# Layer 0's start: input in four transfers, idle products on the identity, constants of layer 1 later, SyncE in the source's order

## The chip, the cores and the metric

The kernel runs on one core of one Trainium2 chip. A core has a matrix engine (TensorE, PE), a vector engine (VectorE, DVE), an activation engine (ScalarE, ACT), a general one (GpSimd, POOL) and a sync engine (SyncE, SP) that mostly issues transfers (DMAs). Each engine works through its own list of instructions in order, and waits on semaphores that the other engines and the DMAs raise. The metric is the device time of one execution in microseconds (us); less is better.

## What is computed

Two transformer layers on an input of 4 sequences x 512 tokens x 256 features, all in float32:

```
x = x + L0_attn(layernorm(x))     causal attention, 16 heads of 16
x = x + L0_ffn(layernorm(x))      router over 8 experts per output feature, top 2
x = x + L1_attn(layernorm(x))     16 query heads of 128, 4 key/value heads
x = x + L1_ffn(layernorm(x))      gated MLP of 2048, weights unpacked from 4 bits
```

The change lies in the start of the first line: the layer norm, the projections to queries, keys and values, and the first scores of the attention.

```
_layernorm(x) = (x - mean(x)) / sqrt(var(x) + 1e-05)
qkv = einsum('bsd,od->bso', x, w_project)
att = softmax(where(causal, -1e9, q . k / sqrt(16)))
out = einsum('bsd,od->bso', att . v, w_out)
```

## The kernel before

The 2048 tokens lie in SBUF as `xres`, 128 partitions x 16 tiles x 256 features. Four tiles make a block (512 tokens); there are four blocks, and block j holds the same 128 positions of all four sequences. Layer 0's attention goes through 44 batches (`batches`): block 0 has four, one for each sequence, with all four groups of heads at once; block 1 has eight; the blocks 2 and 3 have sixteen each.

What every batch does is written as functions: `greatest(n)` computes scores on PE (L652), `mask(n)` adds the causal mask on PE and takes row maxima on DVE (L665, L671), `shift(n)` transposes the maxima and subtracts them from the queries (L681, L684), `powers(n)` computes scores again, exponentials on ACT and the causal cut on POOL (L700, L709, L719), `mixed(n)` multiplies with the values (L736). Between them `fill` takes pieces from other streams: projections of the next block, the folding of the router's biases into its weights (`fold_pieces`, L258, which reads the weights `rw` and `ew`), later the router and expert products.

The order of the work on PE, DVE, POOL and ACT is that of the source: `tc.manual_schedule` over these four engines (L72) is open from L72 to L1179. SP is not among them before the change: the framework's scheduler places its transfers, except that the expert weights' transfers keep their order among themselves (`load_pair`, L531). In the compiled list of SP, this leads to the order: half of block 0's input, half of the projection weights `wp`, block 1's input, `wo`, block 2's input, four transfers of `rw`, block 3's input, three of the biases `bs`, four of `ew`, then the transfers of queries and keys (`qk`) of block 0 (eight on SP, eight on ACT's queue), block 1's first eight, four of `rw`, eight of `qk`, four of `ew`.

The start, before the first batch, goes as follows.

- The input of block 0 is loaded in two transfers of two tiles each, one by SP and one by ACT (L65, L66), then `wp` in two halves (L460).
- POOL makes the identity `ident`; DVE makes small constants, among them `mask32` (L86), `fold8` (L91) and `mask8` (L95). The last two are used in layer 1 only. POOL writes `qk` blanks (L482, L486), `ident_h` and `later` (L489 to L492). DVE fills the values' ones (`va`, L481) and clears `bs` (L497), into which the biases are loaded (L499).
- PE computes three idle products of `ident` with `wp` (L800). Each float32 product is shown as two records.
- DVE takes statistics of four tiles (L180, L181), adds epsilon (L184), POOL takes the power -1/2 (L185), DVE normalizes the tiles (L194, `xn`); PE transposes (L210), ACT copies to `xT` (L582). The same norm follows at once for block 1.
- POOL: `blanks`, then `blank(1, i)` (L476, L474), then the split of the biases into three bfloat16 parts (`split_biases`, L518 to L529).
- `projections(0, xT)`: for each of two halves two products (`project`, L545), evicted by ACT into `stage` (L549) and sent by eight transfers into `qk` (L555), four issued by SP and four by ACT; then two value products (`values`, L567), evicted by ACT (L573). PSUM has two buffers for all of these (`ps_dn`, L100), so that a product waits for the eviction of the last but one.
- `inputs_T(1, ...)` transposes block 1 (copied by DVE, L582), then `greatest(0)`, `mask(0)`, and the batches begin.

Of the kernel before, what the change touches and what calls it, by code (L numbers as in the profile page):

```python
# [32 lines left out]
def tile_transformer(  # L33
# [40 lines left out]
    make_identity(nc, ident)  # L74
    minus_half = const.tile([P, 4], F32, name="minus_half")
# [19 lines left out]
    nc.vector.tensor_copy(mask8, fold8.unsqueeze(1).to_broadcast([P, NS, 8]))  # L95

# [352 lines left out]
    with ExitStack() as l0:  # L449
# [32 lines left out]
        nc.gpsimd.tensor_copy(  # L482
            qk[:, :, 0].rearrange("p g s q -> p g (s q)"),
            mask32[:, :4].unsqueeze(2).to_broadcast([P, 4, 512]),
# [45 lines left out]

        def load_pair(w, dram, n):  # L531
            e, hc = divmod(n, 2)
            tc.keep_in_program_order(
                nc.sync.dma_start(
                    out=w[:, hc, 2 * e : 2 * e + 2],
                    in_=dram[hc * P : (hc + 1) * P, 2 * e : 2 * e + 2],
                )
            )

        def project(j, xT, half, stage, i):  # L540

            at = 256 * (1 - i) + 128 * half
            ps = ps_dn.tile([P, 512], F32, tag="dn", name=f"qk_ps{j}_{half}_{i}")
            for hc in range(2):
                nc.tensor.matmul(  # L545
                    ps, lhsT=wp[:, hc, at : at + P],
                    rhs=xT[:, hc].rearrange("p s q -> p (s q)"), start=hc == 0, stop=hc == 1,
                )
            nc.scalar.copy(stage[:, i], ps)  # L549
            if i:  # L550
                to = 4 + j % 2
                for r in range(8):
                    h = 32 * (r % 4)
                    eng = nc.scalar if j == 0 and r % 2 else nc.sync
                    eng.dma_start(  # L555
                        out=qk[h + 4 : h + 20, 2 * half + r // 4, j : to + 1 : to - j].rearrange(
                            "p i s q -> p i (s q)"
                        ),
                        in_=stage[16 * r : 16 * r + 16],
                    )  # L560

        def values(j, xT, s):

            ps = ps_dn.tile([P, 2, HID], F32, tag="dn", name=f"v_ps{j}_{s}")
            for i in range(2):
                for hc in range(2):
                    nc.tensor.matmul(  # L567
                        ps[:, i], lhsT=xT[:, hc, s + i], rhs=wp[:, hc, 512:768],
                        start=hc == 0, stop=hc == 1,
                    )  # L570
            at = j * per_block
            to = va[:, at : at + per_block].rearrange("p (s h d) -> p s h d", s=NS, d=17)
            nc.scalar.copy(  # L573
                to[:, s : s + 2, :, 0:16], ps.rearrange("p s (h d) -> p s h d", d=16)
            )

# [13 lines left out]
        def projections(j, xT):  # L590
            if j > 1:
                for s in (0, 2):
                    yield need("PE", 1.75, 1, cond=lambda: blanked > 5 * j - 10)
                    values(j, xT, s)
            for half in range(2):
                if j > 1 and half:

                    stage = b1.tile(
                        [P, 2, 512], F32, tag="hi4" if j == 2 else "part", name=f"stage{j}_1"
                    )  # L600
                elif j or half:
                    stage = a1.tile([P, 2, 512], F32, tag="stage", name=f"stage{j}_{half}")
                else:
                    stage = unused("stage0", "p (i q) -> p i q", i=2)
                for i in range(2):

                    yield need(
                        "PE", 1.75, 0 if half or i else 1,
                        cond=lambda: j < 2 or done >= 8 * j - 12 and blanked >= 5 * j - 5,
                    )  # L610
                    project(j, xT, half, stage, i)
                if half == (not j) and j < 2:
                    for s in (0, 2):
                        yield need("PE", 1.75)
                        values(j, xT, s)

        def prepare(j):

            out = []
            yield from norm_pieces(  # L620
                j, b1, b2, out, cond=lambda: j == 2 or inputs[2].next is None
            )
            xT = a1.tile([P, 2, NS, P], F32, tag="xT0", name=f"xT0_{j}")
            yield from inputs_T(j, out[0], xT)
            yield from projections(j, xT)

        def unused(name, pattern, **sizes):
# [168 lines left out]


        ps = ps_mm.tile([P, 4, P], F32, tag="mm", name="idle")
        for i in range(3):
            nc.tensor.matmul(  # L800
                ps.rearrange("p b q -> p (b q)"), lhsT=ident, rhs=wp[:, 0, :512],
                start=not i, stop=i == 2,
            )
        load_x(1)
        nc.sync.dma_start(out=wo, in_=w_out.rearrange("(k p) o -> p k o", p=P))
        both = [[], []]
        for j in range(2):
            for piece in norm_pieces(j, b1, b2, both[j]):
                pass
            normed.clear()  # L810
            if not j:
                blanks(both[0][0])
                xT = a1.tile([P, 2, NS, P], F32, tag="xT0", name="xT0_0")
                for piece in inputs_T(0, both[0][0], xT):
                    pass
# [6 lines left out]
        for piece in inputs_T(1, both[1][0], xT):  # L822
            pass
        greatest(0)
        mask(0)
# [7 lines left out]
        for n in range(NBT):  # L833
# [473 lines left out]
```

## Time and profile before

| | us |
|---|---|
| median of 3 runs (1169.44 to 1170.32) | 1169.55 |
| the profiled execution's time | 1170.3 |
| its span | 1168.6 |
| PE busy | 1142.0 |
| DVE busy | 809.8 |
| ACT busy | 484.3 |
| POOL busy | 108.4 |
| first statistics of block 0 (DVE) | 5.96 |
| first projection of block 0 (PE) | 13.51 |
| first maxima of the first batch (DVE) | 28.79 |

The profile is of one execution. The span runs from its first instruction to its last; the profiled execution's own time is 1.7 us longer than its span and 0.75 us above the median. A row of the timeline has the start and the duration in us, the engine, the line of the source, the operation, its output and inputs, the shape and a count; the last bracket is the idle time of that engine before it and what ended the wait. Where several instructions are merged the duration is that from the first start to the last end. "PEld" is PE's loading of weights, "SPq" and "ACTq" are issues of transfers. In the rows of DMA issues "us to landing" is counted from the issue. The granted clock of PE in the profile is 1.00 in every stretch of 10 us looked at in the first 120.

### The profile page before, as it was taken

Reading aid. Unit: us, or ns where it says so; the run is one execution under the profiler, and the core shown is the slowest. Engines: PE = TensorE matmul, PEld = TensorE weight load, DVE = VectorE, ACT = ScalarE, POOL = GpSimd, SP = SyncE. Lnnn points to the kernel's source line nnn. Section 1 sums busy time; section 2 is a strip of 40 time slices with the busy share of each in tenths; the row PEclk is TensorE's granted clock in tenths of the full one; section 3 lists DMA queues with packets and bytes.
Section 4 is the critical chain, followed back from the end, with each engine's and each line's share of the span. In section 5 each row is a group of like instructions: output and inputs, shape, how many; then the busy total and the mean of one; then the engine's idle time right before and its main releaser. Section 6 shows DMA issues by size and latency. Waiting matters only on the chain.

```text
span 1168.6 us, 18563 instructions
## 1 busy us (share of the span) xinstructions
PE 1142.0 (98%) x7178; PEld 661.5 (57%) x7178; DVE 809.8 (69%) x1783; ACT 484.3 (41%) x1099; POOL 108.4 (9%) x152
## 2 busy tenths in 40 slices
PE   7999999999999999999999999999999999999998
PEld 3666555556554445555555555566644475484487
DVE  5676889999988953868773785687699845716710
ACT  1444645556555542444443444544344312303300
POOL 7322221212112000000000000000000000000000
PEclk9999999999999999999999999999999999999999
DMA  7230110000000500000000001120110000000000
GB/s 219 64 83 2 19 20 2 2 1 2 2 2 1 181 1 1 1 1 1 1 1 1 1 1 46 28 54 21 27 46 1 0 1 19 0 1 19 1 18 19
DMA packets 21239, 26.46 MB, mean 23 GB/s; under 512 B 5128, under 2 KB 14600, under 8 KB 21152
## 3 DMA queue, kind: packets, MB, share of 16 engines
q1 hardware_dynamic: 20480, 24.10, 7.5%
q10 hardware_dynamic: 672, 1.18, 0.4%
q8 instruction: 56, 0.92, 0.3%
q14 instruction: 31, 0.25, 0.1%
HBM read 18.97 MB, written 2.10 MB: 18 GB/s over the span
## 4 chain that ended last, share of the span: by engine, by line
PE 81%; DVE 13%; ACT 2%; issue 1%; POOL 1%; DMA 0%; SPq 0%; ACTq 0%; DVEq 0%; POOLq 0%
PE qk_ps L987 11%; PE y L1234 9%; PE o L1078 9%; PE g L916 9%; PE u L916 9%; PE lg_ps L234 8%; PE eo L234 7%; PE s L652 3%; PE s L700 3%; DVE mx L671 3%; PE av L736 2%; PE v_ps L969 2%; PE qk_ps L545 2%; PE a L1058 1%; PE s L1000 1%
## 5 line engine op out<-in xcount | busy, mean ns | idle before, releaser
L987 PE MATMUL qk_ps<-xT,wqkv 128*128 128x512 f32 x320 | 148.9, 599 | 2.3 <-ACT part L323 1.2
L234 PE MATMUL lg_ps<-rw,xT 128*128 128x512 f32 x256 | 122.5, 601 | 1.4 <-ACT xT L954 0.3
L234 PE MATMUL eo<-ew,xT 128*128 128x512 f32 x256 | 121.5, 600 | 0.8 <-ACT lg L297 0.5
L1078 PE MATMUL o<-wpj,oT 128*128 128x256 f32 x512 | 119.1, 382 | 0.0
L1234 PE MATMUL y<-wd,it 128*128 128x256 f32 x512 | 111.8, 379 | 0.0
L1078 PEld LDWEIGHTS o<-wpj,oT 128*128 128x128 f32 x512 | 95.9, 190 | 27.5 <-issue 14.3
L1234 PEld LDWEIGHTS y<-wd,it 128*128 128x128 f32 x512 | 97.0, 190 | 15.0 <-issue 2.2
L671 DVE TENSOR_REDUCE mx<-s 128x1 f32<-128x384 f32 (+3 forms) x176 | 100.4, 632 | 1.3 <-PE s L665 1.3
L987 PEld LDWEIGHTS qk_ps<-xT,wqkv 128*128 128x128 f32 x320 | 59.1, 190 | 71.4 <-issue 57.4
L709 ACT ACTIVATE pt<-s 128x512 f32<-128x512 f32 (+1 forms) x176 | 84.1, 563 | 35.3 <-PE s L700 35.3
L916 PE MATMUL g<-xT,wgu 128*128 128x512 f32 x192 | 90.4, 593 | 0.0
L916 PE MATMUL u<-xT,wgu 128*128 128x512 f32 x192 | 90.2, 592 | 0.0
L323 ACT ACTIVATE part<-eo,c 128x256 f32<-128x256 f32 x128 | 53.7, 472 | 85.2 <-PE eo L234 75.2
L719 POOL TENSOR_SCALAR_AFFINE_SELECT pt<-pt 128x256 f32<-128x256 f32 (+2 forms) x88 | 63.2, 725 | 249.8 <-ACT pt L709 249.3
L1212 ACT ACTIVATE th<-sq 128x512 f32<-128x512 f32 x64 | 40.3, 630 | 87.6 <-DVE sq L1211 87.6
L234 PEld LDWEIGHTS lg_ps<-rw,xT 128*128 128x128 f32 x256 | 46.1, 190 | 46.1 <-issue 37.3
L234 PEld LDWEIGHTS eo<-ew,xT 128*128 128x128 f32 x256 | 46.1, 190 | 45.7 <-issue 38.3
L222 DVE TENSOR_TENSOR xres<-xres,y 128x256 f32<-128x256 f32 x16 | 6.7, 421 | 92.5 <-PE y L1234 92.5
L185 POOL TENSOR_TENSOR ln_rs<-rs_v,minus_half 128x4 f32<-128x4 f32 x16 | 17.6, 1099 | 552.2 <-DVE rs_v L184 439.9
L297 ACT COPY lg<-lg_ps 128x512 f32<-128x512 f32 x64 | 37.6, 588 | 73.5 <-PE lg_ps L234 73.5
L1213 DVE SCALAR_TENSOR_TENSOR th<-th,g 128x512 f32<-128x512 f32 x63 | 43.2, 686 | 29.2 <-ACT th L1212 29.2
L916 PEld LDWEIGHTS u<-xT,wgu 128*128 128x128 f32 x192 | 36.5, 190 | 45.9 <-issue 44.7
(233 smaller groups left out, 1776.8 us busy)
## 6 DMA issues: line engine op xcount, KB each, us to landing
qk<-stage SPq DMA_DIRECT2D x56, 64.0 KB, 2.4
wqkv<-in_w_qkv SPq DMA_DIRECT2D x8, 320.0 KB, 6.8
rw<-in_router_w SPq DMA_DIRECT2D x8, 256.0 KB, 7.8
ew<-in_expert_w SPq DMA_DIRECT2D x8, 256.0 KB, 4.6
wpj<-in_w_proj SPq DMA_DIRECT2D x1, 2048.0 KB
out<-xres SPq DMA_DIRECT2D x4, 512.0 KB, 2.6
xres<-in_x SPq DMA_DIRECT2D x3, 512.0 KB, 9.0
dq_wgu<-in_gate_w SPq DMA_DIRECT2D x8, 128.0 KB, 2.4
```

The source lines that it names most:

```text
L234: nc.tensor.matmul(ps, lhsT=xT[:, hc, (g % 4) * P : (g % 4 + 1) * P], rhs=w[:, hc, 2 * pair : 2 * pair + 2, :].rearrange("p e o -> p (e o) ...
L297: nc.scalar.copy(lg[:, 2 * pair : 2 * pair + 2, :].rearrange("p e o -> p (e o)"), ps)
L323: nc.scalar.mul(part[:, e % 4], ps[:, i], c[:, e : e + 1])
L671: nc.vector.tensor_reduce(maxes[n % 2][:, h, gs[0] : gs[0] + nb], ps[:, : nb * nk].rearrange("p (b k) -> p b k", b=nb), AX.X, ALU.max,)
L709: nc.scalar.activation(pt[:, i, : nb * nk], tiles[2 * pair + i][:, : nb * nk], AF.Exp, scale=0.25)
L719: nc.gpsimd.affine_select(out=last, in_=last, compare_op=ALU.is_ge, fill=0.0, base=0, pattern=pattern, channel_multiplier=-1,)
L916: nc.tensor.matmul(ps, lhsT=wgu[:, w, half, jj, par * P : (par + 1) * P], rhs=xT[:, half, :], start=half == 0, stop=half == 1,)
L987: nc.tensor.matmul(ps, lhsT=wqkv[:, hc, kv, h, :], rhs=xT[:, hc, :], start=hc == 0, stop=hc == 1,)
L1078: nc.tensor.matmul(ys[t // 2][:, t % 2], lhsT=state["o"][:, h, t * P : (t + 1) * P], rhs=wpj[:, HPK * kv + h, :], start=kv == 0 and h == 0 ...
L1212: nc.scalar.activation(th, sq, AF.Tanh, scale=0.7978845608028654)
L1213: nc.vector.scalar_tensor_tensor(th, th, 1.0, gp, ALU.add, ALU.mult)
L1234: nc.tensor.matmul(ps, lhsT=it[:, c // 2, c % 2, t * P : (t + 1) * P], rhs=wd[:, c // 2, c % 2, :], start=c == 0, stop=c == 2 * NJ - 1,)
```

## The change

- Block 0's input goes in four transfers of one tile, by SP and ACT in turn.
- SP is put in the source's order too, from the constants on until batch 3 (`loads_in_order`); `load_pair` loses its own ordering.
- `fold8` and `mask8` are computed behind the evictions of block 0's values, ahead of the copies of block 1's `xT`.
- The idle products are five, of `ident` with `ident` repeated four times; they read no weights.
- Block 0's norm becomes `normed_by_twos`: statistics of two tiles, epsilon, POOL's power for those two, the same for the other two, then four `xn`.
- The clearing of `bs`, the biases' transfers and the filling of `va` come behind block 0's transposes in the source, so behind `xn` on DVE.
- Block 1's statistics are written ahead of block 0's projections of half 0, its `xn` behind them. PE's own order stays what it was.
- Block 0's projections of half 1 and its values are evicted by DVE, no longer by ACT. On DVE these four evictions stand behind block 1's `xn`.
- Block 2's input is loaded behind block 0's projections, block 3's in batch 2. As the loads now stand in source order, SP's list becomes: two tiles of block 0, half of `wp`, block 1's input, `wo`, three of `bs`, eight `qk` of block 0, block 2's input, eight `qk` of block 1, eight of `rw`, eight `qk`, four of `ew`, block 3's input, four of `ew`, and from there on as before.

```diff
-    for t, eng in ((0, nc.sync), (2, nc.scalar)):
-        eng.dma_start(out=xres[:, t : t + 2, :], in_=x[:, t : t + 2, :])
+    for t in range(4):
+        eng = nc.scalar if t % 2 else nc.sync
+        eng.dma_start(out=xres[:, t, :], in_=x[:, t, :])
...
+    loads_in_order = ctx.enter_context(ExitStack())
+    loads_in_order.enter_context(tc.manual_schedule(engines={mybir.EngineType.SP}))
...
-    nc.vector.tensor_reduce(
-        fold8, ident.rearrange("p (t b) -> p b t", b=8), AX.X, ALU.add
-    )
-    nc.vector.tensor_copy(mask8, fold8.unsqueeze(1).to_broadcast([P, NS, 8]))
...
-        nc.vector.memset(va[:, :per_block], 1.0)
...
-        nc.vector.memset(bs, 0.0)
-        for i in range(3):
-            nc.sync.dma_start(out=bs[32 * i : 32 * i + 8], in_=bias)
...
-            nc.scalar.copy(stage[:, i], ps)
+            (nc.scalar.copy if j or not half else nc.vector.tensor_copy)(stage[:, i], ps)
...
-            nc.scalar.copy(
+            (nc.scalar.copy if j else nc.vector.tensor_copy)(
                 to[:, s : s + 2, :, 0:16], ps.rearrange("p s (h d) -> p s h d", d=16)
             )
...
+        def normed_by_twos():
...
+            for two in (slice(0, 2), slice(2, 4)):
+                for t in range(two.start, two.stop):
+                    nc.vector.bn_stats(st[:, t, :], xres[:, t, :])
+                    nc.vector.bn_aggr(mv[:, t, :], st[:, t, :])
...
+                nc.vector.tensor_scalar(v, mv[:, two, 1], EPS, None, ALU.add)
+                nc.gpsimd.tensor_tensor(rs, v, minus_half[:, :2], ALU.pow)
+                roots.append(rs)
+            for t in range(4):
+                nc.vector.tensor_scalar(
+                    xn[:, t, :], xres[:, t, :], mv[:, t, 0:1],
+                    roots[t // 2][:, t % 2 : t % 2 + 1], ALU.subtract, ALU.mult,
+                )
...
-        for i in range(3):
+        for i in range(5):
             nc.tensor.matmul(
-                ps.rearrange("p b q -> p (b q)"), lhsT=ident, rhs=wp[:, 0, :512],
-                start=not i, stop=i == 2,
+                ps, lhsT=ident, rhs=ident.unsqueeze(1).to_broadcast([P, 4, P]),
+                start=not i, stop=i == 4,
             )
...
+        xn = normed_by_twos()
+        blanks(xn)
...
+        nc.vector.memset(bs, 0.0)
+        for i in range(3):
+            nc.sync.dma_start(out=bs[32 * i : 32 * i + 8], in_=bias)
+        nc.vector.memset(va[:, :per_block], 1.0)
+        second = []
+        norm_1 = norm_pieces(1, b1, b2, second)
+        for _ in range(3):
+            next(norm_1)
+        firsts_0 = projections(0, xT)
+        for _ in range(3):
+            next(firsts_0)
+        for piece in norm_1:
+            pass
...
-        for piece in projections(0, xT):
+        for piece in firsts_0:
             pass
+        load_x(2)
+        nc.vector.tensor_reduce(
+            fold8, ident.rearrange("p (t b) -> p b t", b=8), AX.X, ALU.add
+        )
+        nc.vector.tensor_copy(mask8, fold8.unsqueeze(1).to_broadcast([P, NS, 8]))
...
-            if n in (0, 2):
-                load_x(n // 2 + 2)
+            if n == 2:
+                load_x(3)
+            if n == 3:
+                loads_in_order.close()
```

More of the change, by code (lines that the diff above doesn't have):

```diff
@@ L532, in load_pair @@
             e, hc = divmod(n, 2)
[L533 to L537, printed above, removed]
+            nc.sync.dma_start(
+                out=w[:, hc, 2 * e : 2 * e + 2],
+                in_=dram[hc * P : (hc + 1) * P, 2 * e : 2 * e + 2],
             )
@@ L625, in prepare @@
             yield from projections(j, xT)
+        def normed_by_twos():
+            xn = b1.tile([P, 4, HID], F32, tag="xn", name="xn0_0")
+            st = b2.tile([P, 4, 6], F32, tag="ln_st", name="ln_st0_0")
+            mv = b2.tile([P, 4, 2], F32, tag="ln_mv", name="ln_mv0_0")
+            roots = []
+            for two in (slice(0, 2), slice(2, 4)):
+                for t in range(two.start, two.stop):
+                    nc.vector.bn_stats(st[:, t, :], xres[:, t, :])
+                    nc.vector.bn_aggr(mv[:, t, :], st[:, t, :])
+                v = b2.tile([P, 4], F32, tag="rs_v", name=f"rs_v0_{two.start}")[:, :2]
+                rs = b2.tile([P, 4], F32, tag="ln_rs", name=f"ln_rs0_{two.start}")[:, :2]
+                nc.vector.tensor_scalar(v, mv[:, two, 1], EPS, None, ALU.add)
[6 more added lines that the diff above has]
+                )
+            return xn
         def unused(name, pattern, **sizes):
@@ L805, in tile_transformer @@
         nc.sync.dma_start(out=wo, in_=w_out.rearrange("(k p) o -> p k o", p=P))
[L806 to L815, printed above, removed]
+        xn = normed_by_twos()
+        blanks(xn)
+        xT = a1.tile([P, 2, NS, P], F32, tag="xT0", name="xT0_0")
+        for piece in inputs_T(0, xn, xT):
+            pass
[11 more added lines that the diff above has]
+        for piece in norm_1:
+            pass
+        normed.clear()
         for i in range(5):
@@ L818, in tile_transformer @@
         split_biases()
-        for piece in projections(0, xT):
+        for piece in firsts_0:
             pass
+        load_x(2)
[3 more added lines that the diff above has]
+        nc.vector.tensor_copy(mask8, fold8.unsqueeze(1).to_broadcast([P, NS, 8]))
         xT = unused("xT0_1", "p (h s q) -> p h s q", h=2, s=NS)
-        for piece in inputs_T(1, both[1][0], xT):
+        for piece in inputs_T(1, second[0], xT):
             pass
```

## The prediction

> **What bounds the kernel now.** I read the page first, then the opening of the timeline, then the chain and the waits in the same stretch. The page says that the kernel is one long TensorE (PE) program:
>
> ```profile
> span 1168.6 us, 18563 instructions
> PE 1142.0 (98%) x7178; PEld 661.5 (57%) x7178; DVE 809.8 (69%) x1783; ACT 484.3 (41%) x1099; POOL 108.4 (9%) x152
> ```
>
> PE is busy 98% of the span, and the diff alters its list of instructions in one place only: three idle products become five. So nothing can be won from PE's work. What can be won is time ahead of it. The timeline of the first 32 us (start, duration, engine, line) shows that opening:
>
> ```profile
> 1.90 1.89 POOL L482 COPY qk<-mask 128x2048 f32<-128x2048 f32 x1 [0.53 <-DVE mask L86]
> 2.16 3.42 DVE L95 COPY mask<-fold 128x32 f32<-128x32 f32 x1
> 3.73 1.80 POOL L486 MEMSET qk<- 128x2048 f32 x1
> 5.96 0.36 DVE L180 BATCH_NORM_STATS2 ln_st<-xres 128x6 f32<-128x256 f32 x1
> 7.12 5.27 PE L800 MATMUL idle<-wp,ident 128*128 128x512 f32 x6 [7.12 <-DMA wp<-in_w_project]
> 8.40 1.02 POOL L185 TENSOR_TENSOR ln_rs<-rs_v,minus_half 128x4 f32<-128x4 f32 x1 [2.13 <-DVE rs_v L184]
> 9.46 1.38 DVE L194 TENSOR_SCALAR xn<-xres,ln_mv,ln_rs 128x256 f32<-128x256 f32 x4 [1.14 <-POOL ln_rs L185]
> 12.23 1.04 PE L210 MATMUL x_ps<-ident,xn 128*128 128x128 f32 x8
> 13.51 7.13 PE L545 MATMUL qk_ps<-xT,wp 128*128 128x512 f32 x16 [0.24 <-DMA xres<-in_x]
> 14.31 2.52 DVE L194 TENSOR_SCALAR xn<-xres,ln_mv,ln_rs 128x256 f32<-128x256 f32 x4 [1.13 <-POOL ln_rs L185]
> 20.91 1.07 ACT L549 COPY stage<-qk_ps 128x512 f32<-128x512 f32 x2 [3.08 <-DMA qk<-stage]
> 22.02 2.80 ACTq L555 DMA_DIRECT2D qk<-stage  x4
> 24.91 1.07 ACT L573 COPY va<-v_ps 128x512 f32<-128x512 f32 x2 [2.93 <-DMA qk<-stage]
> 26.63 1.81 PE L652 MATMUL s<-qk 32*128 32x128 f32 x32
> 28.79 2.48 DVE L671 TENSOR_REDUCE mx<-s 128x4 f32<-128x512 f32 x4 [1.26 <-PE s L665]
> ```
>
> Three losses are to be seen. The first statistics start at 5.96 although the two halves of the input were issued at 0.8 and took 4.0 to 4.2 us to land, so at about 5.0: VectorE (DVE) was held by the 128x32 copy of L95, which took 3.42 us and ended with POOL's memset (5.53). The transposes start at 12.23 although xn was ready at 10.84: six passes of idle products stand ahead of them, begun only when the projection weights had landed (7.12). And ScalarE (ACT) evicts the third projection and the values 3.08 and 2.93 us late, because it is issuing four DMAs each time. The chain names the same items: mask L95 for 3.42 us, then DMA qk<-stage for 3.00. From the first maxima (28.79) on, the order on PE and the waits are those of both kernels, so I carry the sum to that point and compare there.
>
> **The change, part by part.**
>
> *Input in four, DVE cleared.* Two more issues of 0.4 us; the weights wp are issued 0.42 later, land at about 7.4 instead of 7.0, and are needed after 10. DVE loses L91, L95 and both memsets ahead of the statistics and is free at 1.84, so the landing binds. The two halves, 0.5 MB, landed near 4.9; the DMA view of the first 30 us shows 376 GB/s in that stretch, so half the bytes are there 0.7 us sooner: an estimate of 4.2 for the first pair, 4.9 for the second. Four statistics with their aggregation take 2.15 us in the old timeline (5.96 to 8.11). In two pairs, each behind its transfer, they end near 6.6, the first pair at 5.4.
>
> *The root in two.* POOL's own queue is untouched: L482, L486, L489 to L492 end at 6.27. So the first root cannot start before 6.3, whatever the input does. One of 128x4 costs 1.02; one of 128x2 is not in the trace. It lies between half (0.5) and the full 1.02; I take 0.9, nearest to the measured row, so that the pair ends at 8.1 (7.3 to 8.4). Here a rule speaks against the split. The Trainium skill (SBUF — State Buffer, Who interferes with whom) says that a VectorE copy or tensor_scalar in its two-port mode and a GpSimd instruction exclude each other for a whole instruction. The row that bears on it: xn takes 1.38 for four at 9.46 with POOL idle and 2.52 at 14.31 beside four POOL copies. By an undisturbed row the first two xn would pass beside the second root and all four end at 8.8; by the rule they wait for it and end at 8.1 + 1.38 = 9.5. I take the rule: 9.5 (8.7 to 9.8).
>
> *Idle products on the identity.* Ten passes, which wait only for ident (1.4). The old six ran 0.86 us apart up to 12.2, twice the 0.43 of the projections, so PE came to full pace 4.4 to 5.1 us after its first product. With four to eight slow passes the ten end between 7.5 and 9.2: off the path, and cost nothing while xn is the later. If all ten stayed slow they would end at 10.0 and cost 0.5. In the chain block 2 shows 1.05 us between the end of its last xn (50.96) and its first projection (52.01). So the projections start at 9.5 + 1.05 = 10.55 instead of 13.51: 2.96 us won.
>
> *Memsets of bs and va moved behind xn.* On the chain they are worth 0.5 each, as rows 0.91 and 0.96: 1.0 to 1.9, I take 1.2. From the end of xn of block 0 to the start of xn of block 1 the old kernel needs 3.47 (10.84 to 14.31). So xn of block 1 runs from 9.5 + 1.2 + 3.47 = 14.2, with POOL's four copies beside it again (2.52), to 16.7. Queued behind it are the new evictions. The bias transfers wait for the memset of bs and stand ahead of the qk transfers on SP; they issue at about 10 to 11, the qk transfers not before 14.9.
>
> *Evictions of half 1 and of block 0's values to DVE.* The third projection is complete 5.45 us after the start: 16.0. DVE takes it at 16.7 (0.65, as its two xT copies at 26.25, 1.29) to 17.35. PE ends the fourth at 10.55 + 7.13 = 17.7 and finds the PSUM buffer free: no wait where the old one lost 0.9. DVE evicts the fourth to 18.45, the values run from 17.75 to 21.45 (3.72), their second eviction ends at 22.15, the transposes of block 1 at 22.75. ACT, with nothing but issues left, starts the second set of qk transfers at 18.45 instead of 22.02; the last of four is issued at 20.65, and with the median of 3.7 us to landing the last scores end near 24.9, with SP's 2.4 near 23.9. I take 24.5, and the first maxima on PE's side at 24.85.
>
> *fold8 and mask8 behind the evictions.* Reduction 0.37, to 22.5. The copy is the 3.42 row again. Uncontended it is under 0.1; here POOL is in the bias split (18.3 to 28.9 in the old timeline, instructions of 0.6 to 1.5). I wait for one of them, as each xn did, and take 1.2: 23.7. Two xT copies: 25.0. So the first maxima come at 25.0: **3.8 us earlier than 28.79**.
>
> *Loads in the source's order.* Nothing is added: 16 weight transfers, of which eight used to go at 3.5 to 15. Block 2's input now goes behind the second qk set (about 21) and is read at 43.9 - 3.8. rw goes behind the first qk transfers of block 1, from about 38.4; its first pair is added to at 54.2 - 3.8 = 50.4, and the longest landing of an rw or ew transfer in the trace is 8.0 after issue, so by about 47.5. ew follows the transfers at 54.7 to 59.8, so from 56; first use 71.5 - 3.8 = 67.7, landing by 65. Block 3's input lies between and is used near 94. Cost nothing, with 3 us of cover; what hides it is block 1's scores. If the cover went, DVE's L258 would hold the maxima queued behind it.
>
> **Sum.** 3.8 us off the profiled execution: its span 1168.6 becomes 1164.8, its time 1170.3 (1.7 around the span) becomes 1166.5. That execution is 0.75 above the median, so I forecast 1169.55 - 3.8 = **1165.8**. The unknowns: xn -0.8/+0.3, landing -0.6/+0.4, memsets up to +0.7, mask8 -1.1/+0.8. Together 1164.2 to 1167.2.
>
> **Rivals.**
>
> *PE cools down again* (9%). The skill (TensorE: Matmul & The Clock Gate, The HAM clock gate) says that the half rate returns after an idle window of about 3.4 us. Idle products that end at 7.5 leave 3.0 us with only transposes before 10.55. The old gap was 1.3 us (12.2 to 13.51), so the trace shows nothing either way. By the row no cost; by the rule in its bad phase 5.1 us at half pace, 2.5 us lost: 1168.3. I take the row, as the gap is under the window.
>
> *The gain is given back at the loads* (9%). If ew or rw land over 7 us later than reckoned, DVE waits at L258 and the start's 3.8 are lost: 1169.5, or beyond. Against it: the 8.0 was met under a heavier load (298 GB/s in the first 10 us) than there will be.
>
> *mask8 locked out to the end of the bias split: slower* (8%). The old copy sat through two POOL instructions. If it sits through all to 28.87, the xT copies end at 30.3 and the maxima start 1.5 us later than now: 1171.1. It decides from the point where mask8 ends after 27.5. Against it: POOL's split waits for its own results with gaps of 0.06 to 0.08, and xn alternated one for one with POOL at 14.31 and at 47.45.
>
> *Chances.* Forecast 74%; the change is measurable from about 0.2%, 2.3 us, so below 1167.2. Faster 0.76 (the forecast, and a mild case of cooling), same 0.19 (cooling, most of the loads' case, mask8), slower 0.05 (a loads' case worse than reckoned). The range 1164.2 to 1168.6 takes in the forecast and cooling.
>
> **What would show it.** First statistics near 4.2 and not 5.96; roots at 6.3, 7.2; xn ending at 9.5; projections at 10.55; values at 17.75 without a wait; ACT's second issues at 18.45; mask8 near 1 us; first maxima at 25.0; all later rows shifted by one constant; no DVE wait at L258. I am wrong if the projections' passes run 0.86 apart, if mask8 ends after 25, or if the shift at 100 us differs from that at 30.

## The result and the profile after

| | before | after |
|---|---|---|
| median (runs) | 1170.26 (12) | 1166.9 (12) |
| range of the runs | 1169.03 to 1170.85 | 1166.59 to 1169.71 |
| profiled execution, its span | 1170.3, 1168.6 | 1166.64, 1164.9 |
| first projection of block 0 | 13.51 | 9.60 |
| first maxima | 28.79 | 24.87 |

The ratio after to before is 0.9976 [0.9969, 0.9984]: 2.8 us faster by the ratio, 3.4 by the medians, 3.7 by the two profiled executions. Ten of the twelve runs lie between 1166.59 and 1167.00; the other two, 1168.25 and 1169.71, come back below. The forecast was 1165.8, range 1164.2 to 1168.6.

The head of the page of after, first its span and the busy time of each engine, then the granted clock in tenths over the span's 40 slices:

```profile
span 1164.9 us, 18575 instructions
...
PE 1144.1 (98%) x7182; PEld 662.6 (57%) x7182; DVE 812.4 (70%) x1788; ACT 481.9 (41%) x1095; POOL 108.2 (9%) x153
...
PEclk9999999999999999999999999999999999999999
```

PE has four records more (two idle products), and 2.1 us more of busy time in a span that is 3.7 shorter. The gain is time ahead of PE's work. The opening in the timeline of after (start, duration, engine, line; last bracket: idle time before it and what ended it):

```profile
1.43 6.68 PE L816 MATMUL idle<-ident 128*128 128x512 f32 x10 [1.43 <-POOL ident masks.py:199]
...
3.50 0.43 DVE L629 BATCH_NORM_STATS2 ln_st<-xres 128x6 f32<-128x256 f32 x1 [1.66 <-DMA xres<-in_x]
...
4.71 0.86 DVE L633 TENSOR_SCALAR rs_v<-ln_mv 128x2 f32<-128x2 f32 x1
...
6.26 1.51 POOL L634 TENSOR_TENSOR ln_rs<-rs_v,minus_half 128x2 f32<-128x2 f32 x2
...
7.00 1.54 DVE L637 TENSOR_SCALAR xn<-xres,ln_mv,ln_rs 128x256 f32<-128x256 f32 x4 [0.47 <-POOL ln_rs L634]
...
9.60 7.13 PE L539 MATMUL qk_ps<-xT,wp 128*128 128x512 f32 x16 [0.24 <-ACT xT L576]
...
13.99 6.41 SPq L549 DMA_DIRECT2D qk<-stage  x8
14.01 6.83 ACTq L549 DMA_DIRECT2D qk<-stage  x8
...
14.17 2.52 DVE L194 TENSOR_SCALAR xn<-xres,ln_mv,ln_rs 128x256 f32<-128x256 f32 x4 [1.12 <-POOL ln_rs L185]
...
16.61 1.27 DVE L543 COPY stage<-qk_ps 128x512 f32<-128x512 f32 x2
...
17.34 3.72 PE L561 MATMUL v_ps<-wp,xT 128*128 128x256 f32 x16 [0.60 <-DVE stage L543]
...
22.11 1.41 DVE L850 COPY mask<-fold 128x32 f32<-128x32 f32 x1
...
22.43 2.08 PE L668 MATMUL s<-qk 32*128 32x128 f32 x32
...
24.87 2.48 DVE L687 TENSOR_REDUCE mx<-s 128x4 f32<-128x512 f32 x4 [0.16 <-PE s L681]
```

Two things are to be seen against the opening of before. Nothing now stands between the last xn and its transposes: the idle products end at 8.11, xn at 8.54, the projections follow 1.06 later, 3.91 us earlier than in before. And the shift is nearly the same further on. PE waits 0.60 at the values, where before waited 0.91, because the third eviction stands on DVE behind block 1's xn; so the values start 4.21 earlier, and the scores 4.20. The scores then take 2.08 us and not 1.81, which brings the shift to 3.92 at the first maxima; the trace shows no wait of PE in them. From there it stays: 3.92 at the products of 107.83 us in before (103.91 in after), 3.83 at the last addition.

### The profile page after: what moved, and what is told of

The parts are those of the page before. It is cut to its first block, busy times and chain, and to the rows that moved or that the text cites. A ratio compares the mean times of both kernels' runs of the same rounds, so it can differ in the third digit from the quotient of the medians.

```text
span 1164.9 us, 18575 instructions
## 1 busy us (share of the span) xinstructions
PE 1144.1 (98%) x7182; PEld 662.6 (57%) x7182; DVE 812.4 (70%) x1788; ACT 481.9 (41%) x1095; POOL 108.2 (9%) x153
## 4 chain that ended last, share of the span: by engine, by line
PE 82%; DVE 13%; issue 2%; ACT 1%; POOL 1%; SPq 0%; DMA 0%; POOLq 0%; DVEq 0%; ACTq 0%
PE qk_ps L1019 11%; PE y L1266 9%; PE o L1110 9%; PE g L948 9%; PE u L948 9%; PE lg_ps L234 8%; PE eo L234 7%; PE s L668 3%; PE s L716 3%; DVE mx L687 3%; PE av L752 2%; PE v_ps L1001 2%; PE qk_ps L539 2%; PE a L1090 1%; PE s L1032 1%
## 5 line engine op out<-in xcount | busy, mean ns | idle before, releaser
L687 DVE TENSOR_REDUCE mx<-s 128x1 f32<-128x384 f32 (+3 forms) x176 | 100.5, 633 | 0.2 <-PE s L681 0.2
L185 POOL TENSOR_TENSOR ln_rs<-rs_v,minus_half 128x4 f32<-128x4 f32 x15 | 16.6, 1103 | 552.2 <-DVE rs_v L184 440.0
```

The source lines that it names most:

```text
L687: nc.vector.tensor_reduce(maxes[n % 2][:, h, gs[0] : gs[0] + nb], ps[:, : nb * nk].rearrange("p (b k) -> p b k", b=nb), AX.X, ALU.max,)
```

## The experiments

All kernels are edits of the kernel after or of the kernel before. Each was run 7 to 21 times between runs of before; the numbers in brackets behind a median are the range of its runs, those behind a ratio to before its 95% interval. A trace is of one execution of each, so a first maximum is one reading and a median is many. "First maxima" is the start of the first row of L687 (L671 in before), at whatever line the edit moves it to.

**1. The old idle products** in the kernel after (u_idle):

```diff
-                ps, lhsT=ident, rhs=ident.unsqueeze(1).to_broadcast([P, 4, P]),
+                ps.rearrange("p b q -> p (b q)"), lhsT=ident, rhs=wp[:, 0, :512],
```

with three products instead of five.

> The changed kernel with the old idle products: three of ident with the projection weights. Theory of the chain: what stands ahead of the first maxima is what counts, and PE's idle products are the largest item. wp lands at about 6.7, six slow passes of 0.86 end at 11.8, the projections start at 13.1 instead of 9.60, the fourth product ends 3.5 later and its eviction 3.0 later (DVE has 0.5 of waiting to give): first maxima at 27.8 instead of 24.87, time 1166.9 + 2.9 = 1169.8. Rival (loads): the traffic of the first 20 us is what was won, and the idle products are as good as hidden: first maxima within 0.5 of 24.87, time 1167.2.

Measured: 1170.41 (1169.68 to 1173.69), ratio 1.0009 [1.0001, 1.0017]. The timeline of u_idle:

```profile
7.05 4.66 PE L816 MATMUL idle<-wp,ident 128*128 128x512 f32 x6 [7.05 <-POOL ln_rs L634]
...
12.82 7.13 PE L539 MATMUL qk_ps<-xT,wp 128*128 128x512 f32 x16 [0.24 <-ACT xT L576]
...
28.00 2.48 DVE L687 TENSOR_REDUCE mx<-s 128x4 f32<-128x512 f32 x4 [1.96 <-PE s L681]
```

xn was ready at 8.53 as in after, but the old products held PE to 11.71. They read `wp`, issued at 1.74 at the latest and landed up to 5.2 us later; the bracket names POOL's ln_rs, which they do not read. The projections come 3.22 us later than in after, the first maxima 3.13, and by the median the whole gain is gone. The idle products are the gate. Behind it the rest of the change brings the first maxima 0.79 forward (28.00 against 28.79), of which the medians show nothing. The runs scatter widely, and two of the three above 1171.5 have a mean granted clock of 1.000, so not all of that scatter is the clock's.

**2. fold8 and mask8 in front again** (u_mask8): the two statements back to where before has them.

> The changed kernel with fold8 and mask8 back ahead of the first statistics. Theory of the chain: the 128x32 copy sits out POOL's copy and memset again (to 5.5), the first statistics start at 5.6 instead of 3.50, xn ends at 9.4 instead of 8.54, and everything on DVE up to the third eviction moves by 0.9; behind it 1.4 us of the copy are gone, but there PE's scores bind. First maxima at 25.8, time 1166.9 + 0.9 = 1167.8. Rival (the lock beside the bias split costs as much as it saves): first maxima at 24.9 or earlier, time 1166.9.

Measured: 1167.52 (1167.36 to 1170.71), ratio 0.9984 [0.9975, 0.9992]. The timeline of u_mask8:

```profile
2.17 3.40 DVE L99 COPY mask<-fold 128x32 f32<-128x32 f32 x1
3.74 1.83 DVE L633 BATCH_NORM_STATS2 ln_st<-xres 128x6 f32<-128x256 f32 x1
...
10.53 7.13 PE L543 MATMUL qk_ps<-xT,wp 128*128 128x512 f32 x16 [0.24 <-ACT xT L580]
...
25.95 2.48 DVE L691 TENSOR_REDUCE mx<-s 128x4 f32<-128x512 f32 x4 [1.80 <-PE s L685]
```

The first statistics take 1.83 and not 0.43: they are queued behind the 3.40 us copy. The projections come 0.93 later than in after, the maxima 1.08. So moving the masks is worth 1.1 us there, the second share; by the medians it is 0.6.

**3. Block 0's evictions on ACT again** (u_evict):

```diff
-            (nc.scalar.copy if j or not half else nc.vector.tensor_copy)(stage[:, i], ps)
+            nc.scalar.copy(stage[:, i], ps)
...
-            (nc.scalar.copy if j else nc.vector.tensor_copy)(
+            nc.scalar.copy(
```

> The changed kernel with all evictions of block 0 on ACT again. Theory of the chain: in the changed kernel DVE is held by xn of block 1 until 16.7 anyway; ACT issues its first four transfers from 14.0 to 17.0, evicts the third product to 17.6 and the fourth to 18.2 (now 17.88), then issues until 21.2 and evicts the values after that: the last transfer is issued 0.3 later, the transposes of block 1 end 0.4 later. First maxima at 25.2, time 1167.2: of the 3.9 us at the first maxima the move of the evictions is worth 0.3. Rival (the two waits of ACT in the old timeline, 3.08 and 2.93 us, come back in full): first maxima at 27.8, time 1169.8.

Measured: 1166.59 (1166.47 to 1168.16), ratio 0.9972 [0.9962, 0.9982]. ACT's first late eviction in u_evict, and the values and maxima behind it:

```profile
16.75 1.07 ACT L543 COPY stage<-qk_ps 128x512 f32<-128x512 f32 x2 [2.77 <-DMA qk<-stage]
...
17.39 3.72 PE L561 MATMUL v_ps<-wp,xT 128*128 128x256 f32 x16 [0.60 <-ACT stage L543]
...
24.85 2.48 DVE L687 TENSOR_REDUCE mx<-s 128x4 f32<-128x512 f32 x4 [1.45 <-PE s L681]
```

The wait of 0.60 is the same, only its owner differs: ACT comes free of its four issues at 16.75, DVE of block 1's xn at 16.61. The move of the evictions is worth nothing that these runs show; my expected 0.3 us was wrong.

**4. SP's transfers placed by the scheduler again** (u_loads), the rest as in after:

```diff
-    loads_in_order.enter_context(tc.manual_schedule(engines={mybir.EngineType.SP}))
```

with `load_pair` keeping its own order and the inputs of blocks 2 and 3 where before has them.

> The changed kernel with SP left to the scheduler again: block 2's and 3's input, four rw and four ew stand ahead of the biases and of the first qk transfers. Theory as predicted (the loads cost and bring nothing): first maxima at 24.9, time 1166.9. Second theory, from the list of waits: the qk transfers of block 0 wait for the landing of the ew transfers[...] (issued near 11 to 14, landing 5 us later), so they go out 2 us late on SP, and the last scores with them: first maxima at 26.5 to 27, time 1168.7. Rival (loads): the lighter traffic is the whole gain: 28.8, 1170.5.

Measured: 1171.54 (1169.55 to 1172.74, 21 runs), ratio 1.0013 [1.0006, 1.0019]: slower than before. I had forecast for this part that it costs nothing and brings nothing; the second theory above named the wait and had it too small. First a row of SP's waits in u_loads (us in total, times, longest), then the issues of qk in its timeline:

```profile
SPq L549 <- DMA ew<-in_expert_w: 2.7, 2, 1.7
...
15.31 8.74 ACTq L549 DMA_DIRECT2D qk<-stage  x8
...
15.96 6.37 SPq L549 DMA_DIRECT2D qk<-stage  x8
```

Then PE in the timeline of u_loads:

```profile
22.42 0.72 PE L668 MATMUL s<-qk 32*128 32x128 f32 x14
23.48 0.49 PE L668 MATMUL s<-qk 32*128 32x128 f32 x4 [0.33 <-DMA qk<-stage]
24.48 0.49 PE L668 MATMUL s<-qk 32*128 32x128 f32 x4 [0.51 <-DMA qk<-stage]
25.39 1.55 PE L668 MATMUL s<-qk 32*128 32x128 f32 x10 [0.42 <-DMA qk<-stage]
26.87 1.89 PE L681 MATMUL s<-later,ident_h 128*128 128x512 bf16 x4
```

The issues of qk on SP wait twice until a transfer of `ew` is done, and start at 15.96 instead of 13.99. Those on ACT start at 15.31 instead of 14.01 and end at 24.05 instead of 20.84; for them the trace names no wait. PE gets the queries and keys in pieces. It is the issues that are late, not the transfers that are slow: from issue to landing the median is 3.4 us on SP and 3.6 on ACT, in after 3.1 and 3.8. The first maxima come at 27.51, 2.64 later than in after. A second cost shows in the last row: four masks take 1.89 where after has 1.04. The table by stretches of u_loads (length, busy times, granted clock, DMA share, GB/s) names it. In its second row the clock, third from the end, is 0.50:

```profile
20.00:26.00 6.00, 4.32 (x41) 2.97 (x40) 2.41 (x6) 0.00 (x0) 5.60 (x7) 1.00 0.75 124
26.00:32.80 6.80, 6.80 (x46) 4.18 (x47) 3.32 (x6) 0.00 (x0) 3.70 (x10) 0.50 0.01 2
```

The clock is half for 6.8 us. The span is 4.2 longer than that of after: 2.64 up to the first maxima, and 1.6 behind them (4.21 is reached by 110 us).

**5. Does the half clock cost by itself?** u_loads with filler products where PE waits (u_loads_fill), behind the first three groups of the first batch's scores:

```diff
+                if not n and b in (0, 1, 2):
+                    idle = ps_mm.tile([P, 2, P], F32, tag="mm", name=f"idle_{b}")
+                    nc.tensor.matmul(
+                        idle, lhsT=ident, rhs=ident.unsqueeze(1).to_broadcast([P, 2, P]),
+                        start=True, stop=True,
+                    )
```

> u_loads (the kernel after, with SP's transfers placed by the scheduler as before) with the same three products between the score products of the first batch, where PE waited 0.3 to 0.5 us for each group's queries and keys, and the clock was half from 26.0 to 32.8 us. Two-cost theory (late transfers 2.6 us, half clock 1.6 us): first maxima as in u_loads, 27.5 to 27.9, clock 1.00, the end 1.6 us earlier: 1169.6 to 1170.2 against 1171.54. Rival, one cost (the transfers alone make all 4.2 us, and the half clock lies beside other waits): time stays at 1171 to 1172 with the clock at 1.00. Third: the products are too few to hold the clock, it is half again, time 1171.5 to 1172.

Measured: 1168.86 (1168.24 to 1170.63), ratio 0.9991 [0.9983, 0.9999]. The same two stretches in u_loads_fill:

```profile
20.00:26.00 6.00, 5.18 (x41) 3.42 (x40) 3.30 (x6) 0.00 (x0) 5.42 (x6) 1.00 0.85 131
26.00:32.80 6.80, 6.57 (x55) 3.98 (x54) 3.88 (x7) 0.00 (x0) 4.58 (x12) 1.00 0.01 2
```

The clock stays whole, and the kernel is 2.7 us faster than u_loads by the medians, although its first maxima are 0.5 later (28.01). So there are two costs, and the clock's is the greater by the medians: at least 2.7, more than the 1.6 that I expected, with about 2.0 left between u_loads_fill and after. In the one execution that was profiled of each the sizes differ (1.25 between them): how long the clock stays low varies from run to run (mean granted clock 0.995 to 0.998 in the runs of u_loads, 0.999 to 1.000 with the fillers).

**6. to 8. Parts alone, in the kernel before:** the new idle products (idle_alone), SP in the source's order (loads_alone), both (idle_loads).

> The kernel before with the new idle products alone (five of ident with itself, from 1.4 us on). Theory of the chain alone: xn is ready at 10.84, the projections start at 12.1 instead of 13.51, everything behind them moves by 1.4: first maxima at 27.4 instead of 28.79, time 1170.0 - 1.4 = 1168.6. Theory with the loads: ew is issued at 11.5 to 15.2 and lands up to 20 us, and the qk transfers[...] wait for it, so they can't go out 1.4 earlier: first maxima between 28.2 and 28.8, PE waits for them in pieces and may fall to half pace: 1169.4 to 1171.

> The kernel before with the loads in the source's order alone. Both theories: the first qk transfers wait for the third and fourth product and for ACT's own issues[...] (in the old timeline they go out 0.05 us behind the eviction at 17.84), so the order of the loads brings next to nothing: first maxima at 28.3 to 28.8, time 1169.5 to 1170. Rival (the lighter traffic is a gain of its own): first maxima at 27 or earlier, 1168 or less.

> The kernel before with the two together. Theory with the loads: the projections at 12.1 and nothing in front of the qk transfers, so the 1.4 us come through: first maxima at 27.3, time 1168.5; the two together are worth more than the sum of each alone. Theory of the chain alone: the same as the idle products alone.

| | median (range) | ratio | first maxima |
|---|---|---|---|
| idle_alone | 1169.84 (1168.37 to 1170.28) | 0.9996 [0.9988, 1.0004] | 27.08 |
| loads_alone | 1169.76 (1168.78 to 1170.67) | 1.0 [0.9992, 1.0008] | 28.32 |
| idle_loads | 1168.66 (1168.49 to 1170.41) | 0.9996 [0.9988, 1.0004] | 27.13 |

Two rows of the timeline of idle_alone:

```profile
11.90 7.13 PE L545 MATMUL qk_ps<-xT,wp 128*128 128x512 f32 x16 [0.24 <-ACT xT L582]
...
27.08 2.48 DVE L671 TENSOR_REDUCE mx<-s 128x4 f32<-128x512 f32 x4 [1.36 <-PE s L665]
```

In the profiled execution the idle products alone bring the maxima 1.71 forward, 0.3 more than the chain said: PE's gate moves from 12.2 to the end of xn (10.85). The loads' order alone does next to nothing, and adds nothing to the idle products at the first maxima. In idle_alone the qk transfers go out at 16.29, right behind their eviction, although the four transfers of `ew` land only from 16.6 on; SP waits 0.2 us for one of them. In the kernel after, where qk is ready at 14, the old order costs 2.7 us of waiting on SP (u_loads).

None of the three ratios is clear of 1. The runs of idle_alone fall into two groups, six at 1168.37 to 1168.72 and seven at 1169.84 to 1170.28, and so do those of idle_loads, seven at 1168.49 to 1168.66 and six at 1169.89 to 1170.41; the medians differ by which group has one run more. The upper group has lost the gain. In idle_alone it has a mean granted clock of 0.999 against 1.000, but in idle_loads 0.999 stands in both groups, and the two fastest runs of loads_alone have 0.998. So the cause of the two groups is open; no run of an upper group was profiled.

**9. A shorter start still** (best2): after, with POOL's memset of L485 behind the first xn, the fills of `bs` and `va` on ACT, POOL's copies waiting for block 1's xn, the masks of layer 1 in batch 0, four idle products.

> The changed kernel with what its trace still shows ahead of the first maxima taken away: POOL's memset of a qk slot (L485) behind xn of block 0, so that the roots start when the statistics are there and not at 6.26; the clearing of bs and the filling of va on ACT, which is idle from 3.5 to 9; POOL waits for block 1's xn before its blanks, so that these stop alternating with xn; mask8 in the first batch; four idle products instead of five. Theory of the chain: roots at 4.8 and 5.7, xn at 7.3 instead of 8.54, projections at 8.4 instead of 9.60; xn of block 1 at 12 to 13.5, so the third eviction starts when its product ends, at 13.9 instead of 16.61, the fourth at 15.6, the transposes end at 20.5 and the first maxima stand at 22.6 instead of 24.87: time 1166.7 - 2.3 = 1164.4. Rival (transfers and PE's pace bind): the qk transfers land no more than 1 us earlier and PE waits for them at half pace: 1166 to 1168.

Measured: 1168.1 (1165.63 to 1169.0), ratio 0.9975 [0.9964, 0.9986]. The first maxima come at 24.29, only 0.58 earlier than in after, and not at 22.6: PE reaches the scores at 21.00, 1.43 earlier, and then waits for landings. The first transfer of qk goes out at 13.43, 0.56 earlier than in after. The rival was right. Three runs lie at 1165.63 to 1165.73, four at 1168.1 to 1169.0. The profile is of one of the four, with half the clock from 25.4 on; at 108 us it is 2.3 later than after. Two rows of its timeline and one stretch:

```profile
13.43 6.53 SPq L557 DMA_DIRECT2D qk<-stage  x8
...
24.29 2.48 DVE L695 TENSOR_REDUCE mx<-s 128x4 f32<-128x512 f32 x4 [2.49 <-PE s L689]
...
25.40:32.20 6.80, 6.69 (x38) 4.23 (x37) 4.80 (x10) 0.00 (x0) 3.80 (x11) 0.50 0.00 1
```

**10. best2 with the three fillers** of experiment 5 (best3).

> best2 with three products of the identity with two copies of itself (0.43 us each) put on PE between the score products of the first batch, behind the first, second and third group of heads. There PE waits for the queries and keys to land (0.6 us in three waits). Clock theory (PE's sparse work while it waits lets the granted clock fall to half for 6.8 us from 25.4 on): the clock is 1.00 in all stretches, first maxima at 24.3 to 25.0 (best2 24.29), the masks of the second batch take 1.0 us and not 1.91, and all runs lie at 1165.6 to 1166.4, none near 1168 to 1169. Rival, that the late rows of best2 come from something else than PE's sparseness (the transfers themselves, or a clock that follows some other rule): half of the runs stay at 1168 to 1169, the slow stretch remains.

Measured: 1166.93 (1166.64 to 1167.01), ratio 0.9973 [0.9962, 0.9983]. No run of seven is near 1168, and the clock of the profiled one is 1.00 in every stretch between 20 and 34 us. The timeline of best3:

```profile
21.08 0.50 PE L676 MATMUL s<-qk 32*128 32x128 f32 x8
21.51 0.70 PE L683 MATMUL idle<-ident 128*128 128x256 f32 x2
...
25.13 2.48 DVE L701 TENSOR_REDUCE mx<-s 128x4 f32<-128x512 f32 x4 [3.25 <-PE s L695]
```

The first maxima are back at 25.13: the fillers cost 0.84, all that the shorter start had won. It is no faster than after. The clock theory fits the scatter of best2, as far as seven runs of each can show; the time that I expected (1165.6 to 1166.4) was too low by the fillers' own price.

**11. Three idle products** (idle_3): `range(5)` to `range(3)` in after.

> The kernel after with three idle products, not five; they end near 6.2 us, so PE has next to nothing until the transposes at 7.9 and the projections at 9.6. It tests the prediction's rival that PE cools between idle products and projections, where five left no trace of it. If that gap lets the clock fall: half clock through about 6.8 us from about 8 to 10 on, the projections take 10 to 11 us and not 7.1, first maxima at 27 to 28.5, time 1169 to 1170. If PE need not be busy that closely: clock 1.00, first maxima 24.9, time 1166.6 to 1167, and two of the five products are for nothing.

Measured: 1166.58 (1166.41 to 1168.72), ratio 0.9976 [0.9967, 0.9986]. PE in the timeline of idle_3:

```profile
1.42 5.46 PE L816 MATMUL idle<-ident 128*128 128x512 f32 x6 [1.42 <-POOL ident masks.py:199]
7.46 0.65 PE L210 MATMUL x_ps<-ident,xn 128*128 128x128 f32 x2 [0.57 <-DVE xn L637]
...
9.60 7.13 PE L539 MATMUL qk_ps<-xT,wp 128*128 128x512 f32 x16 [0.24 <-ACT xT L576]
```

The projections start and run as in after. The gap of 2.7 us between idle products and projections, with transposes only, cools nothing, so two of the five products do nothing. Whether the kernel needs any idle product was not tried. Three of nine runs lie at 1167.6 to 1168.7, as two of twelve do in after.

**12. Block 0's norm in one group of four** (one_root):

```diff
-        xn = normed_by_twos()
+        first = []
+        for piece in norm_pieces(0, b1, b2, first):
+            pass
+        normed.clear()
+        xn = first[0]
```

> The kernel after with block 0's norm in one group of four tiles as before (four statistics, one addition of epsilon, one power for four, four xn) and not by twos; input still in four transfers. In after the second root ended at 7.77 and the four xn at 8.54, two of them beside the second root. One power for four tiles starts not before the fourth statistics, about 6.3, and took about 1.4 us before: roots end 7.7 to 8.0, xn end 9.4 to 9.7, projections 10.4 to 10.7 instead of 9.60, first maxima 0.8 to 1.0 later if the chain through the projections sets them (25.7 to 25.9; 1167.5), or 24.9 to 25.1 with 1166.7 if transfers behind it or DVE's fills set the pace.

Measured: 1166.79 (1166.53 to 1170.21), ratio 0.9976 [0.9965, 0.9987]. The timeline of one_root:

```profile
6.25 1.02 POOL L185 TENSOR_TENSOR ln_rs<-rs_v,minus_half 128x4 f32<-128x4 f32 x1
7.30 1.38 DVE L194 TENSOR_SCALAR xn<-xres,ln_mv,ln_rs 128x256 f32<-128x256 f32 x4 [1.32 <-POOL ln_rs L185]
...
9.77 7.13 PE L539 MATMUL qk_ps<-xT,wp 128*128 128x512 f32 x16 [0.24 <-ACT xT L576]
```

I expected 0.8 to 1.0 later; it is 0.17 at the projections and 0.21 at the first maxima (25.08). One root for four takes 1.02 and two roots for two 1.51 in all, so grouping by twos wins little: all four statistics are done before POOL's own queue lets any root begin. That profile has the clock at half from about 27.3 to 30.7, with no wait of PE above 0.6 us in the ten before, and its second maxima at 29.90 against 28.87 in after. In the table by stretches:

```profile
26.00:32.80 6.80, 6.57 (x41) 3.89 (x41) 4.64 (x8) 0.14 (x1) 2.74 (x10) 0.75 0.00 0
```

## Why the prediction was right, point by point

The forecast said 3.8 us off the profiled execution through the first maxima, and 3.92 came. That what stands ahead of the projections is what counts is shown by three runs that undo a part: the projections come 3.22, 0.93 and 0.17 later (u_idle, u_mask8, one_root), the first maxima 3.13, 1.08 and 0.21. That the sum came out within 0.13 is in part luck, as errors of about 0.9 in it cancel. Of its steps:

- **First statistics** near 4.2: 3.50. The quarter transfer lands sooner. It brings nothing, as the roots start at 6.26 (6.3 forecast) behind POOL's queue.
- **Roots** of 0.9 each, ending at 8.1: 0.71 and 0.83, ending at 7.77. Ahead of them, the addition of epsilon took 0.86 instead of 0.17 and ended with POOL's memset; not foreseen, and hidden by the same queue.
- **Idle products** off the path, ending at 7.5 to 9.2: they end at 8.11, and the last xn at 8.54. Their passes start 0.85 apart up to about 5.8 us, 4.4 after the first, and 0.43 apart behind it. Right.
- **xn after the second root (9.5, range 8.7 to 9.8):** wrong. I took the rule over the undisturbed row. The trace has each xn at 0.41, at 7.00, 7.33, 7.80 and 8.13, and the first two lie beside the second root (6.94 to 7.77). The four end at 8.54. The Trainium skill (SBUF — State Buffer, Who interferes with whom) lets a two-port tensor_scalar and a GpSimd instruction exclude each other for a whole instruction; beside this power it did not show, beside POOL's copies at 14.17 it did (2.52 for four). The measurement decides, for each of them, with the reserve that spans on POOL are rough in these profiles. That gave 0.95 us more at the projections: 9.60, not 10.55.
- **Memsets on DVE** at 1.2: from the end of xn to the first statistics of block 1 it is 2.13 (8.54 to 10.67). The term was mis-sized by 0.9. Block 1's xn starts at 14.17, as forecast (14.2), but only since the early xn paid for it.
- **No wait at the values:** wrong, 0.60. PE is 0.95 earlier than reckoned and DVE is not. The wait takes back most of what the early xn gave, and the values start at 17.34 instead of 17.75.
- **ACT's second issues** at 18.45: all eight are issued in one stretch to 20.84 (20.65 forecast for the last), but u_evict shows that this is not where the gain lies. With ACT evicting, the maxima come at 24.85. The move of the evictions was a term of my chain with no worth of its own.
- **mask8** about 1.2: 1.41, through the end of one POOL instruction (L518, to 22.36) and the whole of the next (L519, 22.34 to 23.49). Right in size, and the lock-out that would have made the kernel slower did not come. With no POOL instruction running the same copy took 0.18 (best2), not under 0.1.
- **What ends last:** the forecast had DVE's copies last at 25.0 and PE's side at 24.85. In after the copies end at 24.72, and DVE then waits 0.16 for PE. The two are as near to each other as forecast, in the other order. The 2.4 us to landing that I took for SP is the median over the whole run; near the start it is 3.5 in before and 3.1 in after. It did not decide.
- **Loads "cost nothing":** right as a sum, since no wait for a load stands at L258 in after, as two of its rows show (the first of `rw` and the first of `ew`):

```profile
50.32 1.28 DVE L258 TENSOR_TENSOR rw<-rw,fold 128x512 f32<-128x512 f32 x2 [0.31 <-PE fold L252]
...
67.61 1.27 DVE L258 TENSOR_TENSOR ew<-ew,fold 128x512 f32<-128x512 f32 x2
```

  But "nothing won" was wrong. Once the start is short, the old order makes the qk transfers wait for `ew`, and all is lost and more (1171.54). The order is no gain of its own (loads_alone); in the new kernel the others' gain depends on it.
- **PE cools again:** it does in some kernels' runs, at another place. I had put it between idle products and projections, where after and idle_3 show nothing. The profiles that have it show it behind the first scores, from 25.4 to 27.3 on. The Trainium skill (TensorE: Matmul & The Clock Gate, HAM oscillation — how this bites in real kernels) gives as its abstract rule that PE should have no idle gap above about 3.4 us. No gap there is that long, and the clock falls all the same.

The forecast lies 1.1 us below the median of after. The two sets of runs of before differ by 0.7 in their medians (1169.55 and 1170.26), which is most of that. The profiled execution, forecast at 1166.5, took 1166.64. The other 0.4 is the difference of the medians, 3.4, from the 3.8 that I subtracted; no run here explains it.

**Where the gain comes from**, then: of 3.92 us at the first maxima, the new idle products alone give 1.71. Once they are in, the end of xn is the gate. Moving the masks is worth 1.08 there and grouping by twos 0.2, both measured by taking them out of after. Some 0.9 is left as a difference. It falls to the input in four transfers and the memsets behind xn together, which were not tried apart, and to what the parts do only in company. All of it holds only with the new order of the loads: without it 2.64 of the 3.92 are lost.

**What stays open.** Two runs of after above 1168 are like those of best2 and one_root in size. That they have the same cause is argued, not shown: they were not profiled, and their clock means (0.999, 0.997) decide nothing, as runs of after at 1166.6 and 1166.9 have 0.999 and 0.998. Fillers of 128 rows remove the slow stretch (best3, u_loads_fill). They do two things at once, filling PE's waits and putting other work between the products of 32 rows. That products of 32 rows, much of PE's work just ahead of that stretch and in it, hold the clock less well would fit; neither was tried alone.

## What to carry to other kernels

Products whose only use is to keep an engine busy must not wait for data that come late, and must be done before its real work can start: two of these five were not needed, and the old three cost 3 us. When one gate is opened, look at what the next consumers find in their queues, transfers first: an order of loads that costs nothing in the old kernel may decide in the new one. And undo each part by itself in the new kernel as well as doing it alone in the old one, for the two answers differ (3.13 and 1.71 us for the same idle products).

## What the hardware showed beyond that

- The granted clock fell to half while PE worked in short products and waits of at most 0.6 us. It stayed there for 6.8 us (u_loads, best2) or 3.4 (one_root). The two groups of runs of best2 lie 2.4 us apart; the profile with the half clock is of the slower group, and no run of the faster one was profiled.
- The first passes of PE start 0.85 us apart and come to 0.43 about 4.4 us after the first (after: 1.43 to 5.8), while the granted clock in the profile is 1.00 from the start. So that figure does not show a slow start, and the pace of the passes does.
- The issue of a transfer on SP waited up to 1.7 us for an earlier transfer of other data to be done (`ew` ahead of qk in u_loads), though it reads nothing of it; by what mechanism, the trace does not tell.
- A 128x2 tensor_scalar on DVE took 0.86 instead of 0.17 beside a POOL memset that only writes, while four of 128x256 ran beside or behind POOL's power at 0.41 each.
- The same 128x32 copy on DVE took 0.18 with no POOL instruction running (best2), 0.39 and 0.66 beside one (u_idle, u_evict), 1.41 in after and 3.42 in before, where it sat through more than one. Beside POOL, each of these four copies ended within 0.05 us of the end of a POOL instruction.
